# Two-bank PSUM tiles, two-head score evictions and halved key sums in an fp32 cross-attention block

## The chip, the cores and the metric

One core of a Trainium2 chip runs the whole block in one launch. The metric is the time of one execution in microseconds (us) on the device. Three runs of the kernel before took 665.59, 663.51 and 662.77 us; their median is 663.51.

The core has five engines with an instruction stream each: PE (TensorE, the matrix products; its weight loads are shown as PEld), DVE (VectorE), ACT (ScalarE), POOL (GpSimd) and SP (SyncE, which here only issues DMAs). Each works its stream off in order, and waits on semaphores where an operand comes from another engine. SBUF is the on-chip memory; PSUM holds what PE writes, in eight banks of 128 partitions x 512 fp32 numbers.

## The reference

A cross-attention block with an MLP, all in fp32: `x` is (8, 256, 512), `ctx` is (8, 256, 512), 16 heads of 32.

```python
h   = layer_norm(x, ln1_w, ln1_b)
q   = heads(h   @ q_w + q_b)          # (8, 16, 256, 32)
k   = heads(ctx @ k_w + k_b)
v   = heads(ctx @ v_w + v_b)
att = softmax(where(mask, q @ k.T * HD**-0.5, min)) @ v
hid = merge(att) @ cproj_w + cproj_b + x
y   = gelu(layer_norm(hid, ln2_w, ln2_b) @ fc_w + fc_b)   # (8, 256, 2048)
out = hid + y @ proj_w + proj_b
```

## The kernel before, in words

The eight batches are worked in two halves, g = 0 and 1, of four batches each, in one long program for one core. x and ctx are brought into columns by transposes on PE (`turned`, L709, the matmuls L725: `turn_c0_00` and so on) or through DRAM and DVE (`moved`, L730).

**Products.** Every projection (q, k, v, the output projection o, the MLP's fc and pd) is a Strassen-Winograd product: seven products of quarter operands in place of eight (`quad`, L857), the MLP with two levels of it. Each needs sums of quarters of its operands ahead (names like `c0t1`, `vws1`, `fw0i4_1`, `z1i2_3`, made by `plus`: DVE in one instruction of 1024 columns, L629, POOL in two halves of 512, L627) and sums of its results behind. The results come into PSUM banks called X, Y and W, and `take` (L601) brings them out, on DVE (L629) or on ACT (copies L605, with bias L610). All matmuls are issued at L638, save the transposes at L725 and the warming products at L650, which multiply a constant.

**Attention.** There are 32 units `u` = g, head group, batch: four heads x 256 queries x 256 keys each. `scores` (L1011) takes four one-bank buffers `s{u}_0` to `s{u}_3`, one to a head; a head's scores are keys x queries, in two halves of 128 keys. Eight instructions `ev{u}_jk` (j the head, k the key half; L1019 to L1021, issued by `copy`, L618, on ACT with the key's bias from `cols`) take 128x256 each to the SBUF buffers `pr{u}_0` and `pr{u}_1`, one to a pair of heads, each 128 keys x (2 heads x 2 key halves x 256 queries). Then come the maximum over keys (`mx`, DVE L1024, with `mt`, `mc` on ACT L1033, and `fold` L1034), its way through DRAM to all partitions (`md` out, `mm` back), the subtraction (`less`: DVE L1046 in one instruction of 1024, or POOL L1051 in two of 512) and the exponential (`exp`, ACT L1054). `attend` (L1061) multiplies with ones for the sums (eight matmuls, into the left half of a bank) and with v (eight matmuls, into the right half), and DVE divides (`r`: L1077, L1079, L1080; `att`, L629).

`scores` also has a second kind of unit, "z": there `ss` (L1055 to L1058) first adds the two key halves, as `ss{u}`, and `attend` needs four matmuls with ones in place of eight. In the kernel before, `KINDS` names no such unit.

**Order.** Nothing is scheduled on the chip. `PROGRAM` (L124) is one written list of all operations in order; a word is an operation's name, with a letter for the engine where there is a choice (`less000_0:G` on POOL, `:V` on DVE, `:A` on ACT). Each engine's stream is this list cut down to its own operations. `PLACES` (L350) gives each buffer its slot, and `Order.run` (L94) reads both. `BANKS` (L24) gives the PSUM banks: three of home W and five of home C. `tile_of` (L555) makes each bank one tile `[128, 512]`; a buffer waits until the one that had its bank before has been read.

The names used below: `s000` the score product of unit 000; `av000` its product with ones and v; `o1_0_P6` the sixth product of the output projection of half 1, column half 0; `fc015`, `pd06` parts of the two MLP products; `tq`, `rq` the output and the residual added to it at the end; `c0`, `cq0` the context of half 0 in columns and as loaded; `vw00` a quarter of v's weights.

Of the kernel before, what the change touches and what calls it, by code (L numbers as in the profile page):

```python
# [10 lines left out]
F32 = mybir.dt.float32  # L11
# [12 lines left out]
BANKS = {"W": 3, "C": 5}  # L24
# [19 lines left out]
class Order:  # L44
# [49 lines left out]
    def run(self):  # L94
# [30 lines left out]
cq0_00_1 cq0_00_0 vw00 rows1 cq0_01_1 vw11 vw10 cq0_01_0 turn_c0_10 turn_c0_00 kw00 c0_10:V small cq0_11_0 c0_00:A  # L125
cq0_10_1 rows6 v0_0_P1 rows4 cq0_11_1 vws1:G fw0_00_1 turn_c0_11 fw0_11_1 turn_c0_01 vws2:G rows0 c0_11:V v0_1_P1
c0_01:A kw10 v0_0_t1:A fw0_11_0 c0t1:V fw0_00_0 fw0_10_0 v0_1_t1:A cq0_10_0 turn_c0_31 turn_c0_21 c0_31:V k0_1_P1
c0_21:A c0t2:V rows3 fw0i1_1:G k0_0_P1 fw0_10_1 fw0i4_1:G xt0_0 v0_0_P6 rows8 fw0i4_2:V fw0i4_3:G kws3:V vw01 xt0_7
fw0i4_4:G v0_1_P6 kw11 v0_0_t2:V xt0_6 fw0i1_2:V kw01 fw0i1_4:V c0t3:V v0_0_P5 v0_1_t2:A mk fw0s1:V xt0_2 turn_c0_20
vws4:G fw1_01_1 turn_c0_30 stats_x0_00:V c0_20:A xt0_1 v0_1_P5 c0_30:A fw0s3:V xt0_4 fw0i5_1:G v0_0_P2 v0_1_t3:V  # L130
v0_0_t3:A rows7 kws1:G fw0s2:V xt0_3 fw0_01_0 v0_0_P3 fw0i6_1:V rows2 fw0i7_3:G stats_x0_30:V k0_1_P7 fw1_00_1
v0_0_c12:A xt0_5 stats_x0_31:V stats_x0_01:A fw1_00_0 mk~1 fw0i7_1:V fw1_11_1 v0_1_P2 fw0i6_2:V rows5 fw0i6_4:V
fw0i1_3:V fcd0_7_False stats_x0_11:A fw0i6_3:V qw00 vws3:V v0_1_P3 fw1_10_1 eps_x0_0:V stats_x0_10:V fw1_10_0 pow_x0_0
fcd0_4_True nb_x0_0 eps_x0_1:G fw0i7_2:V k0_1_P2 v0_1_c12:A fw0i7_4:G qw10 fw1i1_3:V stats_x0_20:A kws2:G
stats_x0_21:V cols k0_0_P7 fw1_01_0 cols~1 fcd0_5_False pow_x0_1 fw0i5_3:V k0_1_t1:A fw1_11_0 fw0i5_2:V eps_x0_2:G
k0_0_t1:A eps_x0_3:G k0_0_P2 kws4:V norm_x0_01:A pow_x0_3 fw0_01_1 qw11 pow_x0_2 k0_0_P6 k0_0_c11 fcd0_1_True fw1s3:V
xt1_3 k0_1_P6 nb_x0_3 nb_x0_2 fw1i1_1:V norm_x0_21:A k0_0_t2:V fw1i1_2:G norm_x0_31:A nb_x0_1 k0_0_P5 norm_x0_00:V
fw0i5_4:G k0_1_t2:A v0_0_c11 norm_x0_11:A fcd0_5_True fw1i4_1:V fw1i1_4:V fcd0_7_True norm_x0_30:A k0_1_P5 k0_0_t3:V
fcd1_1_True fw1i4_2:G k0_1_c11 fcd0_6_False fw1s1:G fw1i4_4:V k0_0_P3 k0_1_t3:A xt1_2 norm_x0_10:A k0_0_c22 xt1_0
norm_x0_20:A k0_1_P3 v0_1_c11 k0_0_c12:A fw1i4_3:V c0t4:V turn_x0_00 k0_1_c22 turn_x0_10 x0_00:A turn_x0_11 fw0s4:V  # L140
qw01 qws1:G turn_x0_01 x0_10:A fcd0_6_True turn_x0_20 x0_01:A x0_11:V k0_0_P4 xt1_1 fw1i2_1:V fcd1_5_False fcd1_4_True
fw1s2:V fw1i2_2:G turn_x0_31 k0_1_P4 x0_31:A x0t1:V fcd0_3_False turn_x0_21 fw1i2_4:V turn_x0_30 k0_1_c12:A fw1i2_3:V
q0_1_P1 k0_0_c21 qws2:G fcd1_2_True x0_20:A fcd1_6_False stats_x1_00 x0_21:A fw1i5_3:V fw1i6_1:G kd0_0_12 q0_0_P1
x0_30:A k0_1_c21 fcd1_7_False x0t2:V q0_0_P2 q0_0_t1:A x0t3:G qws3:V kd0_0_21 q0_0_P6 q0_0_c11 fw1i5_1:V cb1_02
fw1i6_3:G s000 q0_0_t2:A cb1_01 stats_x1_01 stats_x1_10 fw1i5_2:G kd0_0_11 q0_0_P5 ev000_20 stats_x1_11 fw1i6_2:G
ev000_10 ev000_00 fw1i5_4:G ev000_30 fw1i6_4:V ev000_01 q0_0_P7 fw1i7_1:G cb1_00 q0_0_t3:A q0_1_t1:A x0t4:G ev000_21
fcd1_5_True q0_1_P6 ev000_31 q0_0_c22 ev000_11 mx000_1 fcd1_6_True fw1i7_2:G q0_0_P4 mx000_0 cb1_12 fw0i2_3:G cb1_10
fw1i7_3:G aggr_x1_00 mt000 aggr_x1_01 kd0_0_22 fw0i2_1:V mc000_3 q0_1_P2 eps_x1_0:G mc000_2 q0_0_c21 mc000_1 fw0i2_2:V
aggr_x1_10 fold000 fw0i2_4:V s020 md000 cb1_11 qws4:G fcd0_2_True fw1s4:G q0_0_P3 cb1_30 ev020_01 q0_0_c12:V ev020_11
fw0i3_3:G fw0i3_1:V q0_1_t2:A fw1i3_3:G ev020_21 q0_1_P5 ev020_31 fw1i7_4:G ev020_30 ev020_00 fw0i3_2:G ev020_10 mm000  # L150
ev020_20 mx020_0 s002 cb1_32 vd0_0_12 v0_1_P7 ev002_30 cb1_03 aggr_x1_11 mx020_1 ev002_21 eps_x1_1:G pow_x1_0 ev002_00
cb1_31 ev002_20 fw1i3_1:G ev002_11 mt020 q0_1_P7 q0_1_c11 ev002_01 pow_x1_1 mc020_3 ev002_31 nb_x1_1 mc020_1
norm_x1_11:V mc020_2 fw1i3_2:V s022 v0_1_c22 fw1i3_4:G fold020 fw0i3_4:G v0_1_P4 nb_x1_0 mx002_1 md020 ev022_00
fcd1_3_True ev002_10 q0_1_t3:A less000_0:G cb1_13 ev022_10 mx002_0 ev022_31 v0_0_P7 ev022_20 ev022_01 ev022_21
q0_1_c22 norm_x1_10:A less000_1:G v0_1_c21 q0_1_P4 mm020 ev022_11 v0_0_c22 ev022_30 cb1_33 mt002 mx022_0 cb1_23 s010
cb1_22 exp000_1 q0_1_c21 cb1_20 v0_0_P4 mx022_1 cb1_21 mc002_1 mc002_2 fcd1_7_True ev010_01 cT1_00 ev010_20 xd1_3
ev010_00 cT1_10 q0_1_P3 mc002_3 ev010_10 kd0_1_12 less020_0:G cT1_11 ev010_31 exp000_0 cT1_01 k1_0_P1 fold002 v0_0_c21
norm_x1_00:A md002 fcd1_3_False q0_1_c12:V ev010_21 vd0_0_11 less020_1:G ev010_11 mt022 k1_1_P1 cT1_30 mc022_1 mc022_3
# [1347 lines left out]
```

## Time and profile before

| | |
|---|---|
| median of three runs | 663.51 us |
| lowest, highest | 662.77, 665.59 us |
| span of the profiled execution | 661.4 us |
| PE busy | 651.4 us, 98% |
| DVE busy | 571.6 us, 86% |
| POOL busy | 450.4 us, 68% |
| ACT busy | 356.5 us, 54% |
| DMA | 146.94 MB, mean 222 GB/s |

The profiled execution's own time isn't recorded apart from its span; the median stands 2.1 us above that span.

How to read the lines that follow. A line of a group reads: source line, engine, operation, out <- in by the program's names, partitions x elements of out and in, how many; then busy us and mean ns of one; then the idle time of the engine just before these instructions, and what ended most of it. A line of the windows gives, for a stretch of the span, each engine's busy us with the number of instructions, the clock granted to PE as a share of full speed, and the DMA engines' busy share and rate. A line of the waits reads: what was waited for, total us, times, longest. A line of the timeline gives start, length, engine, line, operation and how many alike stand in a row. A matmul instruction of fp32 shows as two records, so that a product with ones of eight matmuls stands as x16.

### The profile page before, as it was taken

The page shows a single profiled execution, that of the slowest core. Times are in us where ns is not written, and L with a number is a line of the kernel's source. Part 1 is how long each engine was busy: PE and PEld are TensorE (multiplying, and loading weights), DVE is VectorE, ACT ScalarE, POOL GpSimd, SP SyncE. Part 2 cuts the span into 40 slices and gives each one's busy share as a digit, 9 for nine tenths or more (in the row PEclk, how much of TensorE's full clock was granted, in tenths as well). Part 3 has the DMA queues.
Part 4 walks back from the last instruction along what each step waited for, and adds up shares of the span by engine and source line. Part 5 has one row for each costly group of instructions (what it writes and reads, how often), then busy time and mean ns, then how long its engine had stood idle before and what let it go on. Part 6 is the DMA issues. An engine that isn't in the chain of part 4 may idle for free.

```text
span 661.4 us, 11596 instructions
## 1 busy us (share of the span) xinstructions
PE 651.4 (98%) x3971; PEld 493.3 (75%) x3971; DVE 571.6 (86%) x935; ACT 356.5 (54%) x720; POOL 450.4 (68%) x397
## 2 busy tenths in 40 slices
PE   8999999999999999999999999999999999999997
PEld 6845464477545676787887878888888888888897
DVE  3989799879999999999989989987889779997573
ACT  2365698978989889837688890040222222730000
POOL 2476989868779996988999864659436046314882
PEclk9999999999999999999999999999999999999999
DMA  8999997889888568878555364979999995877256
GB/s 268 323 358 345 228 229 262 287 195 228 236 259 261 174 210 265 270 237 279 163 162 189 129 212 167 304 246 189 192 253 235 247 241 155 179 254 159 49 118 129
DMA packets 216538, 146.94 MB, mean 222 GB/s; under 512 B 125424, under 2 KB 176928, under 8 KB 216480
## 3 DMA queue, kind: packets, MB, share of 16 engines
q1 hardware_dynamic: 216480, 146.21, 78.9%
q8 instruction: 31, 0.51, 0.3%
q14 instruction: 27, 0.22, 0.1%
HBM read 105.67 MB, written 40.50 MB: 221 GB/s over the span
## 4 chain that ended last, share of the span: by engine, by line
PE 52%; DVE 5%; ACT 3%; DMA 1%; issue 1%; POOL 1%; SPq 0%; DVEq 0%
PE fc_X L638 14%; PE pd_X L638 14%; PE pd_W L638 7%; PE fc_W L638 6%; PE pd_Y L638 4%; PE fc_Y L638 3%; PE o_X L638 2%; DVE h L629 1%; PE av L638 1%; ACT pr L1054 1%; PE o_W L638 1%; ACT pr L618 1%; PE s L638 1%; DMA fl<-fcd 1%; DMA qw<-in_L_xattn_cproj_w_dram 1%
## 5 line engine op out<-in xcount | busy, mean ns | idle before, releaser
L618 ACT ACTIVATE pr<-s,cols 128x256 f32<-128x256 f32 x256 | 104.4, 483 | 17.4 <-PE s L638 10.6
L1051 POOL TENSOR_TENSOR pr<-pr,mm 128x512 f32<-128x512 f32 x72 | 98.4, 1393 | 7.7 <-DMA mm<-md 5.2
L1234 ACT ACTIVATE h<-h,cols 128x256 f32<-128x256 f32 x128 | 56.0, 499 | 55.7 <-DVE h L629 54.1
L1024 DVE TRANSPOSE_TENSOR_REDUCE mx<-pr 128x32 f32<-128x1024 f32 x64 | 77.5, 1222 | 2.5 <-ACT pr L618 2.4
L1054 ACT ACTIVATE pr<-pr 128x1024 f32<-128x1024 f32 x64 | 66.6, 1069 | 7.3 <-POOL pr L1051 4.1
L629 DVE TENSOR_TENSOR h<-fc_X,h 128x512 f32<-128x512 f32 x80 | 53.0, 679 | 7.1 <-PE fc_X L638 5.7
L1046 DVE TENSOR_TENSOR pr<-pr,mm 128x1024 f32<-128x1024 f32 x28 | 37.7, 1355 | 0.0
L629 DVE TENSOR_TENSOR h<-fc_W,h 128x512 f32<-128x512 f32 x48 | 32.1, 679 | 5.7 <-PE fc_W L638 5.5
L1033 ACT COPY mx<-mx 32x64 f32<-32x64 f32 x96 | 29.7, 309 | 11.9 <-DVE mx L1030 5.5
L638 PE MATMUL av<-pr,ones 128*32 128x256 f32 x512 | 34.1, 383 | 0.6 <-ACT pr L618 0.5
L610 ACT ACTIVATE e<-pd_X,cols 128x256 f32<-128x256 f32 x7 | 3.3, 471 | 57.0 <-PE pd_X L638 57.0
L629 POOL TENSOR_TENSOR h<-h,fl 128x512 f32<-128x512 f32 x9 | 12.3, 1368 | 25.7 <-DMA out_dram<-tq 22.4
L627 POOL TENSOR_TENSOR z1i<-z1t,z1i 128x512 f32<-128x512 f32 x8 | 10.0, 1270 | 25.5 <-DVE z1i L629 25.5
L638 PEld LDWEIGHTS av<-pr,ones 128*32 128x32 f32 x512 | 14.9, 109 | 16.1 <-issue 5.4
L638 PE MATMUL fc_W<-y1i,fl 128*128 128x256 f32 x100 | 24.5, 380 | 0.0
L638 PE MATMUL fc_X<-y1i,fl 128*128 128x256 f32 x88 | 22.5, 380 | 0.0
L638 PEld LDWEIGHTS fc_W<-y1i,fl 128*128 128x128 f32 x100 | 18.9, 190 | 2.9 <-DVE h L629 0.3
L605 ACT COPY h<-fc_X 128x512 f32<-128x512 f32 x16 | 9.1, 586 | 18.2 <-PE fc_X L638 14.2
L627 POOL TENSOR_TENSOR z1i<-h,z1i 128x512 f32<-128x512 f32 x10 | 13.4, 1362 | 7.8 <-ACT h L1234 4.1
L638 PE MATMUL pd_W<-z0i,pl 128*128 128x256 f32 x80 | 18.6, 379 | 0.0
L638 PEld LDWEIGHTS fc_X<-y1i,fl 128*128 128x128 f32 x88 | 16.7, 190 | 2.5 <-DVE h L629 0.3
L627 POOL TENSOR_TENSOR z0i<-h,z0i 128x512 f32<-128x512 f32 x10 | 16.3, 1653 | 1.4 <-DVE z0i L629 1.2
(601 smaller groups left out, 1905.6 us busy)
## 6 DMA issues: line engine op xcount, KB each, us to landing
mm<-md SPq DMA_DIRECT2D x32, 512.0 KB, 5.1
pl<-prd SPq DMA_DIRECT2D x54, 256.0 KB, 4.4
fl<-fcd SPq DMA_DIRECT2D x40, 256.0 KB, 4.5
fl<-prd SPq DMA_DIRECT2D x23, 256.0 KB, 4.6
fw<-in_L_xattn_fc_w_dram SPq DMA_DIRECT2D x16, 256.0 KB, 5.3
pw<-in_L_xattn_proj_w_dram SPq DMA_DIRECT2D x32, 128.0 KB, 4.2
hid<-in_x_dram SPq DMA_DIRECT2D x8, 512.0 KB, 7.8
hd<-hid SPq DMA_DIRECT2D x8, 512.0 KB, 3.9
```

The costliest lines, as they stand in the source:

```text
L605: (nc.scalar.copy if e == "ACT" else nc.vector.tensor_copy)(to(), of_())
L610: nc.scalar.activation(to(), of_(), AF.Identity, bias=bias(), scale=1.0)
L618: lambda e: nc.scalar.activation(to(), of_(), AF.Identity, bias=bias(), scale=1.0))
L627: nc.gpsimd.tensor_tensor(to()[:, ts(k, 512)], in0()[:, ts(k, 512)], in1()[:, ts(k, 512)], op)
L629: E[e].tensor_tensor(to(), in0(), in1(), op)
L638: nc.tensor.matmul(o(), l(), r(), start=first, stop=True, skip_group_check=True)
L1024: T.op(f"mx{u}_{h}", [("DVE", 1.126)], [(pr[h], None)], [(mx, [h])], lambda e, h=h: nc.vector.tensor_reduce(tile_of(mx)[:, 0:64].rearrange ...
L1033: lambda e, a=a: nc.scalar.copy(turned_()[0:32, 2 * a : 2 * a + 2, :], turned_()[32 * a : 32 * a + 32, 0:2, :]))
L1046: nc.vector.tensor_tensor(p_, p_, m_[:, :, None, :].to_broadcast([P, 2, 2, S]), ALU.subtract)
L1051: E[e].tensor_tensor(p_, p_, at(M, j)[:, None, :].to_broadcast([P, 2, S]), ALU.subtract)
L1054: lambda e, h=h: nc.scalar.activation(tile_of(pr[h]), tile_of(pr[h]), AF.Exp), table="exp")
L1234: lambda e, f=f, b=b, c=c: nc.scalar.activation(at(h[f][b], c), at(h[f][b], c), AF.Gelu_apprx_tanh, bias=col(c_fcb + f * 4 + c), scale=1.0 ...
```

## The change

- `BANKS` becomes four tiles of two banks each (S), whose halves serve as eight banks for everything else (W and C no longer differ). A buffer of kind S takes a whole tile.
- `scores` takes two S buffers `s{u}_0` and `s{u}_1` with two heads each. A unit is evicted by four instructions of 128 x 2 heads x 256 in place of eight.
- `KINDS` names six units "z": 000, 022, 012, 032 and 021 in half 0, 121 in half 1. Their twelve additions of key halves (128x512 each) are put five on DVE, seven on POOL.
- `PROGRAM` and `PLACES` are written anew: another order, other engines for some operations (on DVE 875 program instructions in place of 863, on POOL 296 for 293, on ACT 565 for 696, on PE the same 496 groups), other slots. The list holds no delays, before or now.

```diff
-BANKS = {"W": 3, "C": 5}
+BANKS = {"W": 8, "C": 8, "S": 4}
@@ Order.run
-                    w = where[b.name]
-                    b.home = w[0] if not w[0].isdigit() else b.kind
-                    b.slot = int(w.lstrip("WC"))
+                    b.slot = int(where[b.name])
@@ PROGRAM
-cq0_00_1 cq0_00_0 vw00 rows1 cq0_01_1 vw11 vw10 cq0_01_0 turn_c0_10 turn_c0_00 kw00 c0_10:V small cq0_11_0 c0_00:A
+vw00 cq0_00_1 cq0_00_0 cq0_01_1 cq0_01_0 cq0_11_1 rows7 cq0_11_0 cq0_10_1 cq0_10_0 small turn_c0_00 c0_00:V turn_c0_10
...
@@ KINDS
-KINDS = ("pppppppppppppppp", "pppppppppppppppp")
+KINDS = ("zppzppzzpzpppppp", "pppppppppzpppppp")
@@ tile_of
-    halves = {}
+    halves, sides = {}, {}
...
+            elif b.kind == "S":
+                b.t = banks.tile([P, 1024], F32, tag=f"B{b.slot // 2}", name=b.name)
+                sides[b.slot // 2] = None
             else:
-                b.t = banks.tile([P, 512], F32, tag=f"{b.home}{b.slot}", name=b.name)
+                s, k = divmod(b.slot, 2)
+                if sides.get(s) is None:
+                    sides[s] = banks.tile([P, 1024], F32, tag=f"B{s}", name=b.name)
+                b.t = sides[s][:, ts(k, 512)]
...
-    first = banks.tile([P, 512], F32, tag="W0", name="first")
+    first = banks.tile([P, 1024], F32, tag="B0", name="first")
@@ scores
-        sb = [Buf(f"s{u}_{j}", "C", 2) for j in range(4)]
+        sb = [Buf(f"s{u}_{h}", "S", 4) for h in range(2)]
         mm(f"s{u}", 1.076, [(q[0], None), (k[0], None)], [(s, None) for s in sb], [
-            (lambda kc=kc, j=j: at(sb[j], kc), lambda kc=kc, j=j: row(k, j)[:, ts(kc, P)], lambda j=j: row(q, j), True)
+            (lambda kc=kc, j=j: at(sb[j // 2], 2 * (j % 2) + kc), lambda kc=kc, j=j: row(k, j)[:, ts(kc, P)], lambda j=j: row(q, j), True)
...
-            for j in range(4):
-                copy(f"ev{u}_{j}{kc}", (pr[j // 2], [2 * (j % 2) + kc]), (sb[j], [kc]), lambda j=j, kc=kc: at(pr[j // 2], 2 * (j % 2) + kc),
-                     lambda j=j, kc=kc: at(sb[j], kc), 256, lambda kc=kc: col(2 * (4 * g + b) + kc))
+            for h in range(2):
+                both = lambda t, kc=kc: t.rearrange("p (i k q) -> p k i q", i=2, k=2)[:, kc]
+                copy(f"ev{u}_{h}{kc}", (pr[h], [kc, 2 + kc]), (sb[h], [kc, 2 + kc]), lambda h=h, both=both: both(tile_of(pr[h])),
+                     lambda h=h, both=both: both(tile_of(sb[h])), 512, lambda kc=kc: col(2 * (4 * g + b) + kc))
```

On PE, the place where unit 000 is multiplied with ones and v, before: `s030` is another unit's score product, with its four one-bank buffers, `av000` the unit's own bank.

```order
L638 MATMUL s030_0_1010<-xt0_4_389,k0_1_21_547 128x256
L638 MATMUL s030_1_1012<-xt0_4_389,k0_1_21_547 128x256
L638 MATMUL s030_2_1014<-xt0_4_389,k0_1_21_547 128x256
L638 MATMUL s030_3_1016<-xt0_4_389,k0_1_21_547 128x256
L638 MATMUL av000_1030<-pr000_0_722,ones_91 32x256 x2
L638 MATMUL av000_1030<-pr000_1_718,ones_91 32x256 x2
L638 MATMUL av000_1030<-pr000_0_722,v0_0_11_284 32x256 x2
L638 MATMUL av000_1030<-pr000_1_718,v0_0_11_284 32x256 x2
```

And the same place now. Where a half of a two-bank tile is written, the row has the name of the first buffer that lay in that tile (`v0_0_W`, `ps_c0_00`), and `ss000` is the sum of the two key halves.

```order
L624 MATMUL s012_0_979<-xn_x1_30_946,k0_1_12_604 128x256 x2
L624 MATMUL s012_1_982<-xn_x1_30_946,k0_1_12_604 128x256 x2
L624 MATMUL v0_0_W_807<-ss000_966,ones_91 32x256 x4
L624 MATMUL v0_0_W_807<-pr000_0_709,v0_0_11_350 32x256 x2
L624 MATMUL v0_0_W_807<-pr000_1_719,v0_0_11_350 32x256 x2
L624 MATMUL ps_c0_00_230<-pr020_0_776,ones_91 32x256 x2
```

The score product has two buffers in place of four, and the four rows with ones (each x2) of a unit have become one row x4 on `ss000`; the rows with v are the same.

On ACT, the evictions of unit 000's scores to `pr000_0` and `pr000_1`, before, with those of q products (rows L610, whose target stands in the slot of an old weight, `vw11`, or input, `xt0_7`) among them:

```order
L610 ACTIVATE xt0_7_334<-q0_0_X_673,cols_89 128x512
L618 ACTIVATE pr000_1_718<-s000_2_701,cols_89 128x256
L618 ACTIVATE pr000_0_722<-s000_1_699,cols_89 128x256
L618 ACTIVATE pr000_0_722<-s000_0_697,cols_89 128x256
L618 ACTIVATE pr000_1_718<-s000_3_703,cols_89 128x256
L618 ACTIVATE pr000_0_722<-s000_0_697,cols_89 128x256
L610 ACTIVATE vw11_215<-q0_0_X_673,cols_89 128x512
L610 ACTIVATE xt1_3_529<-q0_1_X_656,cols_89 128x512
L618 ACTIVATE pr000_1_718<-s000_2_701,cols_89 128x256
L618 ACTIVATE pr000_1_718<-s000_3_703,cols_89 128x256
L618 ACTIVATE pr000_0_722<-s000_1_699,cols_89 128x256
```

And now:

```order
L596 ACTIVATE vws1_301<-ps_c0_00_230,cols_89 128x512
L604 ACTIVATE pr000_0_709<-s000_0_699,cols_89 128x2x256
L596 ACTIVATE kws4_477<-ps_c0_00_230,cols_89 128x512
L604 ACTIVATE pr000_1_719<-s000_1_702,cols_89 128x2x256
L604 ACTIVATE pr000_0_709<-s000_0_699,cols_89 128x2x256
L604 ACTIVATE pr000_1_719<-s000_1_702,cols_89 128x2x256
L596 ACTIVATE xt0_1_291<-ps_c0_00_230,cols_89 128x512
```

Eight instructions of 128x256 have become four of 128x2x256, and two evictions with bias stand close to them as before, one of them now ahead of the first score.

On PE, the last attention unit ahead of the second output projection and the projection's first products, before: `av133` is the unit, `o1_0` and `o1_1` the projection, `att1` and `a1t2` its operand and the sums of it.

```order
L638 MATMUL av133_4110<-pr133_1_3933,ones_91 32x256 x2
L638 MATMUL av133_4110<-pr133_0_3920,vws1_255 32x256 x2
L638 MATMUL o1_1_X_4144<-fl013_3_3647,att1_00_2777 128x256 x4
L638 MATMUL o1_0_X_4161<-fl013_3_3647,att1_00_2777 128x256 x4
L638 MATMUL o1_0_Y_4179<-vws1_255,att1_10_3055 128x256 x4
L638 MATMUL o1_1_Y_4189<-vws1_255,att1_10_3055 128x256 x4
L638 MATMUL pd05_X_4197<-z0t1_0_3864,pl01_2_3777 128x256 x4
L638 MATMUL o1_1_X_4144<-fl017_3_3522,a1t2_4202 128x256 x4
L638 MATMUL o1_0_X_4161<-fl017_3_3522,a1t2_4202 128x256 x4
```

And now (the PSUM names are again those of first buffers: the rows with `att1` and `a1t` are the projection's):

```order
L624 MATMUL pd01_X_3607<-pr131_1_3439,ones_91 32x256 x2
L624 MATMUL pd01_X_3607<-pr131_0_3434,vw01_289 32x256 x2
L624 MATMUL pd01_X_3607<-h0_22_3160,pl05_2_3697 128x256 x4
L624 MATMUL fc004_Y_3557<-vws2_303,att1_00_2663 128x256 x4
L624 MATMUL fc005_X_3121<-z0t2_0_3713,v1_1_12_1641 128x256 x4
L624 MATMUL fc004_W_3637<-oxs2_3860,a1t2_3810 128x256 x4
L624 MATMUL fc004_Y_3557<-oxs2_3860,a1t2_3810 128x256 x4
L624 MATMUL fc004_W_3637<-ox10_3829,a1t1_3808 128x256 x4
```

The last unit is 131 in place of 133; one MLP product (`pl05_2`) now stands right ahead of the projection and another (`z0t2_0`) between its first product and those with `a1t2`; of the four rows with `att1` ahead of those only one is left there.

More of the change, by code (lines that the diff above doesn't have):

```diff
@@ L127 @@
[L127 to L146, printed above, removed]
@@ new lines @@
+ps_x0_00=0 x0_00=78 ps_x0_10=1 ps_x0_20=5 x0_10=8 ps_x0_30=7 ps_x0_01=1 x0_01=16 ps_x0_11=0 ps_x0_21=2 x0_11=74
+ps_x0_31=5 c0t1=54 c0t2=44 c0t3=80 c0t4=22 kw00=61 kw01=32 kw10=35 kw11=12 kws1=18 kws2=87 kws3=7 kws4=41 vw00=86
+vw01=37 vw10=28 vw11=53 vws1=82 vws2=71 vws3=20 vws4=29 qw00=36 qw01=56 qw10=40 qw11=65 qws1=44 qws2=43 qws3=45 qws4=42
+x0t1=4 x0t2=34 x0t3=88 x0t4=24 k0_0_X=3 k0_0_11=26 k0_0_Y=0 k0_0_21=19 k0_0_W=3 k0_0_22=77 k0_0_12=57 k0_1_X=4
+k0_1_11=76 k0_1_Y=6 k0_1_21=84 k0_1_W=6 k0_1_22=52 k0_1_12=14 v0_0_X=7 v0_0_11=64 v0_0_Y=1 v0_0_21=50 v0_0_W=0
```

617 lines of the change are left out of this document (307 added, 310 removed).

## The prediction

> **What bounds the kernel now.** I read the page first: its busy line and the clock row.
>
> ```profile
> span 661.4 us, 11596 instructions
> PE 651.4 (98%) x3971; PEld 493.3 (75%) x3971; DVE 571.6 (86%) x935; ACT 356.5 (54%) x720; POOL 450.4 (68%) x397
> PEclk9999999999999999999999999999999999999999
> ```
>
> PE is busy 98% of the span and its clock is granted in full in every slice, so PE's matmul time is the bound: the span shortens where PE gets less work, or where it waits less. The profiled execution's span is 661.4; the median of the three runs is 663.51, so 2.1 us lie around the span. I make the sum on the span and take it from the median. What a measurement of this kernel can tell from no change is about 0.5%, 3.3 us: faster means under 660.2, slower means over 666.8.
>
> An average says nothing of where the slack lies, so the windows came next, cut at the end of the head, where the attention units start, and where PE runs alone with the MLP.
>
> ```profile
> core 0: us, PE busy (x) PEld busy (x) DVE busy (x) ACT busy (x) POOL busy (x), PEclk, DMA share, GB/s
> 0.00:20.00 20.00, 17.43 (x104) 13.96 (x105) 7.75 (x10) 4.12 (x6) 6.56 (x14) 1.00 0.88 281
> 20.00:150.00 130.00, 129.91 (x741) 74.63 (x740) 115.33 (x201) 93.67 (x196) 96.76 (x92) 1.00 0.92 275
> 150.00:310.00 160.00, 156.78 (x1274) 107.06 (x1272) 154.00 (x257) 134.39 (x270) 137.16 (x126) 1.00 0.78 240
> 310.00:400.00 90.00, 89.58 (x621) 71.61 (x618) 82.88 (x134) 73.82 (x142) 76.85 (x61) 1.00 0.58 186
> 400.00:661.00 261.00, 257.72 (x1241) 226.05 (x1239) 211.64 (x337) 50.53 (x109) 133.06 (x107) 1.00 0.80 193
> ```
>
> Length less PE busy gives what PE waits: 2.6 in the head, 0.1, 3.2 from 150 to 310, 0.4, and 3.3 at the end. No better order can return more than these 9.6. DVE is the second bound: from 150 to 310 it is idle 6.0 of 160 us, from 310 to 400 it is idle 7.1 of 90, and from 20 to 150 it is idle 14.7 of 130, together 27.8. ACT is idle 25.6 and POOL 22.8 of the middle 160. The waits of PE say who it is that ends them.
>
> ```profile
> PE ps_c L725 <- DMA cq<-in_ctx_dram: 1.6, 2, 1.2
> PE o_X L638 <- DVE a0t L629: 1.0, 1, 1.0
> ...
> PE s L638 <- DVE q L629: 0.6, 1, 0.6
> PE av L638 <- ACT pr L618: 0.5, 2, 0.4
> PE fc_X L638 <- DVE h L629: 0.4, 2, 0.2
> PE ps_y L725 <- ACT pr L618: 0.3, 1, 0.3
> PE o_X L638 <- DVE a1t L629: 0.2, 1, 0.2
> PE fc_X L638 <- ACT h L605: 0.2, 1, 0.2
> ```
>
> Waits for DVE come to 1.0 + 0.6 + 0.4 + 0.2 = 2.2 us, those for ACT to 0.5 + 0.3 + 0.2 = 1.0.
>
> **The product with ones.** Where the work of PE itself changes is the six units whose sums take halved keys.
>
> ```profile
> 98.18 1.07 PE L638 MATMUL av<-pr,ones 128*32 128x256 f32 x16
> 99.07 1.05 PE L638 MATMUL av<-pr,v 128*32 128x256 f32 x16
> ```
>
> From start to start a unit's whole product with ones takes 99.07 - 98.18 = 0.89 us. Four of the eight matmuls go, 0.445 us, and six units make 2.7 us. This lies on the path, since PE waits for nearly nothing beside it: **-2.7**. No other matmul is added or dropped, so below this stand only waits.
>
> **Evictions of two heads.** ACT moves every score once, before in 256 instructions and now in 128 of twice the size.
>
> ```profile
> L618 ACT ACTIVATE pr<-s,cols 128x256 f32<-128x256 f32 x256 | 104.4, 483 | 17.4 <-PE s L638 10.6
> ```
> ```profile
> L618 ACT ACTIVATE att<-att,cols 128x512 f32<-128x512 f32 x16 | 11.4, 721 | 2.4 <-DVE att L629 2.3
> ```
> ```profile
> 244.98 1.99 ACT L1054 ACTIVATE pr<-pr 128x1024 f32<-128x1024 f32 x2
> ...
> 248.89 3.39 ACT L618 ACTIVATE pr<-s,cols 128x256 f32<-128x256 f32 x9
> ```
>
> Nine evictions in a row take 3.39, so each follows the last after (3.39 - 0.48) / 8 = 0.36 us. Two exponentials of 1024 take 1.99 where one takes about 1.06, a pitch of 0.93. Between 256 at 0.36 and 1024 at 0.93, 512 columns come to 0.55 as an estimate on the straight line: a unit takes 4 x 0.55 = 2.2 in place of 8 x 0.36 = 2.9, 0.7 us less, and 32 units 22 us. The other end is the 721 ns of a 512-wide row of the same form that shows no overlap: 4 x 0.72 = 2.9 and nothing is saved. I take the first, since the new instructions also stand in runs. ACT is at 54%, so neither is on the path; what the path gets is that ACT is late less often. I halve its 1.0 us of waits: **-0.5**, with 0 and -1.0 as bounds.
>
> The change adds a wait here: a score product now needs both banks of a pair, where it took single banks. What is queued behind it is everything, since PE works in order. How often a bank was not free before shows at PE's weight loads:
>
> ```profile
> PEld s L638 <- ACT pr L618: 5.2, 8, 0.8
> ```
>
> Eight times an eviction held up the load of a score product, 0.65 us each, and PE itself showed nothing of it under that name; the load ran ahead of a PE that was still at work. I take 0 for the pairs. The bounds are a further gain of nothing, as nothing was lost on PE, and a loss that the second rival prices.
>
> **DVE and POOL.** The twelve half-key adds go five to DVE and seven to POOL. The order also shifts work between the three engines: on DVE two more subtractions of the maximum, six more evictions of k and q sums, three fewer statistics of x, and seven fewer normalizations.
>
> ```profile
> L1051 POOL TENSOR_TENSOR pr<-pr,mm 128x512 f32<-128x512 f32 x72 | 98.4, 1393 | 7.7 <-DMA mm<-md 5.2
> ...
> L629 DVE TENSOR_TENSOR h<-fc_X,h 128x512 f32<-128x512 f32 x80 | 53.0, 679 | 7.1 <-PE fc_X L638 5.7
> L1046 DVE TENSOR_TENSOR pr<-pr,mm 128x1024 f32<-128x1024 f32 x28 | 37.7, 1355 | 0.0
> ```
> ```profile
> L629 DVE TENSOR_TENSOR c0t<-c,c 128x1024 f32<-128x1024 f32 x2 | 2.4, 1223 | 0.4 <-ACT c L605 0.4
> ```
> ```profile
> L627 POOL TENSOR_TENSOR c1t<-c,c 128x512 f32<-128x512 f32 x4 | 5.0, 1276 | 2.2 <-DVE c L749 2.2
> ```
>
> On DVE: 5 x 0.68 + 2 x 1.36 + 6 x 0.68 - 3 x 0.68 = 8.2; the rest (the normalizations, weight sums, operand sums, one to four instructions in each group) takes 4.8 away by the same means, so DVE has **+3.4 us** ahead of the second output projection. POOL gets 7 x 1.28 = 9.0 and gives two subtractions, in halves 2 x 2 x 1.39 = 5.6, to DVE. Neither is on the path where it can be placed in idle time: the 27.8 us of DVE and 22.8 of POOL. The order gives PE 6.3 us less matmul ahead of that same projection (2.7 of it saved, the rest moved behind it), so DVE must do 3.4 more in 6.3 less. That eats 9.7 of 27.8 and leaves 18: still cover, if it lies where it is needed. The worst stretch decides, so I looked for the run of DVE work that stands most over the PE work beside it: before 162.1 against 157.1, 5.0 over; after 142.5 against 138.4, 4.1 over. By these counts DVE forces less, and of the 2.2 us of waits for DVE I take off in proportion, 2.2 x 0.9 / 5.0 = **-0.4**. The bounds are -2.2 and the third rival.
>
> **Head.** `vw00` is now the first load, the eight context pieces follow, and all their turns but the first pair's stand ahead of the second v product.
>
> ```profile
> 10.10 1.07 PE L725 MATMUL ps_c<-ident,cq 128*128 128x128 f32 x8 [1.17 <-DMA cq<-in_ctx_dram]
> 11.01 1.89 PE L638 MATMUL v_X<-vw,c 128*128 128x256 f32 x8
> 12.74 1.08 PE L725 MATMUL ps_c<-ident,cq 128*128 128x128 f32 x8
> ```
>
> PE waits here for bytes. The wait of 1.17 can go, since the second pair of `cq0` is no longer split by `vw11` and `vw10`: -1.2 at most. On the other side `vw01` is now the twelfth large load, three behind the last context piece: 3 x 0.262 MB at the first window's 281 GB/s land in 2.8 us, and PE has a pair of turns (11.01 - 10.10 = 0.9) and a v product (12.74 - 11.01 = 1.7) to do meanwhile, 2.6. It nearly fits; a late load would cost what such waits cost here, 1.2, and 0.8 if it is the slower of two. I take 0, between -1.2 and +2.
>
> **Tail.** After the last product come an eviction, a transpose back and an add.
>
> ```profile
> L1334 DVE STREAM_TRANSPOSE tq<-po 128x256 f32<-128x256 f32 x32 | 12.8, 424 | 1.0 <-PE pd_X L638 0.8
> ```
> ```profile
> L629 POOL TENSOR_TENSOR tq<-tq,rq 128x512 f32<-128x512 f32 x9 | 11.9, 1330 | 7.1 <-DVE tq L1334 6.4 <-DVE h L629 0.6
> ```
> ```profile
> L629 DVE TENSOR_TENSOR po<-pd_X,po 128x256 f32<-128x256 f32 x20 | 8.3, 415 | 2.9 <-PE pd_X L638 2.6
> ```
> ```profile
> 647.29 1.78 PE pd_X L638 x16
> ```
>
> Ahead of the last products, POOL must add an output (1.33), then two operand sums (2 x 1.28 by the row of halves above): with the eviction and the transpose at 0.42 each, 4.7 us beside three products of 1.78 = 5.3. It fits by 0.6; I take 0, bound +1.
>
> **Sum.** -2.7 - 0.5 - 0.4 + 0 + 0 = -3.6: a span of 657.8 and a time of 663.5 - 3.6 = **659.9**.
>
> **The rivals.** *Pairs of banks.* The four tiles are scarcer than eight banks where score products meet projections; a product that waits for the second bank stops PE. For it speaks the weight-load row above; against it, that the two evictions that freed one bank now free both of a pair. With half of those eight cases, 4 x 0.65 = 2.6 us, reaching PE, the time is 662.5. It decides from about 0.3 us on, where the sum passes 660.2.
>
> *Adds become the bound: slower.* The place is from 150 to 400 us. There the half-key adds have two inputs in SBUF, on both engines, and so have the subtractions. The subtractions, at 1355 against 1223 ns on DVE and 1393 against 1276 on POOL, show 0.12 to 0.13 us of a shared cost each. If DVE sets the time up to the second output projection, PE comes to it 3.4 later than before, whatever it saved, and has 3.6 us of matmul more behind it: 663.5 + 7.0 = 670.5; with half of it, 667.0. It decides once the idle time of DVE from 20 to 400 doesn't come down from 27.8 to below 21 while PE waits for `less`, `ss` or operand sums. Against it stands the worst stretch, 4.1 where it was 5.0. The sharpest form is that each new POOL add stops DVE for its whole 1.28: 7 x 1.28 = 9.0, and 672.5; the 0.13 us of the rows are a tenth of that, so of the slower case I give this form 0.03. The Trainium skill (SBUF — State Buffer, section "Who interferes with whom") holds the rule for it and so speaks against this change: a DVE instruction with two SBUF inputs contends with a GpSimd instruction that reads SBUF, and the one that comes second is blocked outright. By that rule, the rows agree in sign only.
>
> *Nothing happens.* If the six units wait for `ss` as long as they save, the time is 663.5 - 0.9 = 662.6. The adds come between the exponentials and the product and take 0.7 (DVE) or 1.3 us (POOL), but products of other units and projections stand between, so I give it little.
>
> **How the numbers follow.** The sum stands only 0.3 under the line of 660.2, and its case is not all on one side. Its case (the sum right to within its bounds, 656.0 to 662.5) has 0.60: 0.46 below the line, since what I put at nothing in the order is bounded by idle time that it may take back (656.0 is the median less 2.7, less the 3.6 of waits from 150 to 400, less 1.2 of the head), and 0.14 above. Bank pairs have 0.16, nothing happens 0.06: both within 0.5%. Slower has 0.18, half of it over 667.0. So faster is 0.46, same 0.36, slower 0.18. The range is **656.0 to 667.0**: it leaves out the upper half of the slower case, 0.09, and about as much below and between.
>
> **What would show it.** Right: the product with ones at half its count in six units, PE's busy time 2.7 lower, waits of PE for ACT at 0.5, ACT busy 22 lower, the DVE idle from 20 to 400 near 18, no wait of PE for a score eviction over 1 us in sum. Wrong: waits of `s` for `pr` evictions of several us (pairs), or waits of PE for DVE's and POOL's `pr` and `ss` from 150 to 400 of over 4 us (adds), or `ps_c` and `v_X` waits over 4 us in the head.

## The result, and the profile after

The changed kernel takes 806.22 us (median of four runs, 805.68 to 809.11), the kernel before 663.43 on the same chip: a ratio of 1.216, 95% interval 1.213 to 1.219. Forecast were 659.9 and a range up to 667.0. The prediction was wrong by 146 us, and none of its cases held this.

The page of the changed kernel, in the rows that answer to those of before:

```profile
span 804.4 us, 11349 instructions
...
PE 690.4 (86%) x3923; PEld 504.4 (63%) x3923; DVE 579.5 (72%) x944; ACT 343.3 (43%) x603; POOL 442.7 (55%) x398
...
PEclk9999989999999998899999999999999999999999
```

DVE, ACT and POOL have about the work that they had: 579.5 us for 571.6, 343.3 for 356.5, 442.7 for 450.4. They are busy a smaller share of a longer span, so none of them has become the bound. PE is idle 804.4 - 690.4 = 114 us, where it was idle 10, and its busy time has grown by 39 us for 48 records less. The windows, cut as before:

```profile
core 0: us, PE busy (x) PEld busy (x) DVE busy (x) ACT busy (x) POOL busy (x), PEclk, DMA share, GB/s
...
20.00:150.00 130.00, 119.11 (x633) 64.05 (x631) 106.25 (x182) 78.42 (x138) 88.01 (x86) 0.97 0.84 260
150.00:310.00 160.00, 132.68 (x1000) 86.29 (x1000) 123.04 (x206) 109.01 (x181) 103.24 (x94) 0.96 0.61 172
310.00:400.00 90.00, 69.44 (x415) 51.80 (x416) 55.05 (x98) 36.61 (x58) 49.36 (x53) 0.89 0.53 176
400.00:804.00 404.00, 353.00 (x1775) 289.45 (x1773) 287.19 (x453) 110.56 (x208) 197.89 (x157) 0.97 0.64 158
```

From 310 to 400 each of the four engines is idle for a good part: PE 21 of 90 us, DVE 35, ACT 53, POOL 41, though hardly ever all at once (0.1 us of the 90, by the trace). That is the picture of engines that wait for each other in turn, not of a bound. It is no matter of one stage either: after 400 PE loses another 51 of 404. The waits of PE:

```profile
PE fc_X L624 <- DVE h L615: 10.9, 9, 2.5
PE ps_y L624 <- DVE h L615: 8.3, 2, 4.3
PE pd_X L624 <- DVE h L615: 7.7, 7, 2.3
PE av L624 <- DVE rc L1064: 6.1, 1, 6.1
...
PE s L624 <- DVE xt L615: 3.8, 2, 2.9
...
PE s L624 <- DVE h L615: 0.9, 1, 0.9
```

Score products (`s`), the only ones that need both banks of a tile, wait little: with 0.5 for an eviction (`pr`), 5.2 us of PE's 114. And the waits of DVE, to be laid beside the first:

```profile
DVE h L615 <- PE fc_X L624: 21.1, 15, 4.7
DVE h L615 <- PE ps_y L624: 12.1, 6, 5.9
```

PE waits for DVE to read PSUM, and DVE waits for PE to write it. One case shows how. The timeline of PE, and then that of DVE, around the longest wait:

```profile
304.93 1.03 PE L624 MATMUL ps_y<-y0i,fl 128*128 128x256 f32 x4
312.10 2.08 PE L624 MATMUL av<-y,qws 128*128 128x256 f32 x4 [6.14 <-DVE rc L1064]
```
```profile
305.18 0.42 DVE L615 TENSOR_TENSOR att<-av,r 128x256 f32<-128x256 f32 x1 [2.04 <-ACT vws L813]
...
307.91 2.33 DVE L1033 TENSOR_TENSOR pr<-pr,mm 128x1024 f32<-128x1024 f32 x1
...
311.65 0.40 DVE L1064 TRANSPOSE_TENSOR_REDUCE rc<-av 128x8 f32<-128x256 f32 x1
```

In the program the product of 312.10 and the reduction it waits for are these rows:

```
PE   L624 MATMUL av100_2492<-y0_00_2575,qws1_538 128x256 [waits DVE_49]
DVE  L615 TENSOR_TENSOR att1_00_2663<-av100_2492,r100_2621 128x256 [waits DMAHW7_49,Activation_49]
DVE  L1064 TENSOR_REDUCE rc110_2670<-av100_2492 128x8
```

`av100` is the name of a two-bank tile. The product is an MLP product that writes its left bank, columns 0 to 255. The last reader of that bank is `att1_00`, which ended at 305.6. The reduction `rc110` reads the sums of another unit, columns 768 to 1023, in the right bank. It shares no number with the product, but it shares the tile, and the product waits for it: 6.1 us, behind a subtraction of 2.33, two reductions and the queue ahead of them. In the whole program 106 waits of PE are of this sort, for a read of the *other* bank of a tile (80 for DVE, 26 for ACT), and some 95 reads of DVE and ACT wait for a product written to the other bank. These are counts of the program's rows, not of the trace; the program before has none of either.

### The profile page after: what moved, and what is told of

Read it like the earlier page. It is cut to its first block, busy times and chain, and to the rows that moved or that the text cites. A ratio compares the mean times of both kernels' runs of the same rounds, so it can differ in the third digit from the quotient of the medians.

```text
span 804.4 us, 11349 instructions
## 1 busy us (share of the span) xinstructions
PE 690.4 (86%) x3923; PEld 504.4 (63%) x3923; DVE 579.5 (72%) x944; ACT 343.3 (43%) x603; POOL 442.7 (55%) x398
## 5 line engine op out<-in xcount | busy, mean ns | idle before, releaser
L1038 POOL TENSOR_TENSOR pr<-pr,mm 128x512 f32<-128x512 f32 x68 | 88.7, 1329 | 38.7 <-DMA mm<-md 37.3
L604 ACT ACTIVATE pr<-s,cols 128x512 f32<-128x512 f32 x128 | 81.7, 686 | 51.2 <-PE s L624 49.3
L615 DVE TENSOR_TENSOR h<-fc_X,h 128x512 f32<-128x512 f32 x50 | 33.8, 680 | 22.3 <-PE fc_X L624 20.2
L1033 DVE TENSOR_TENSOR pr<-pr,mm 128x1024 f32<-128x1024 f32 x30 | 38.1, 1280 | 1.1 <-DMA mm<-md 1.1
L613 POOL TENSOR_TENSOR z0i<-z0t,z0t 128x512 f32<-128x512 f32 x8 | 12.8, 1620 | 33.3 <-DVE z0t L615 31.5
L615 DVE TENSOR_TENSOR h<-fc_Y,h 128x512 f32<-128x512 f32 x33 | 22.2, 682 | 8.8 <-PE fc_Y L624 7.7
L615 DVE TENSOR_TENSOR h<-pd_X,h 128x512 f32<-128x512 f32 x26 | 17.6, 680 | 7.2 <-PE pd_X L624 6.5
L615 POOL TENSOR_TENSOR tq<-tq,rq 128x512 f32<-128x512 f32 x8 | 10.1, 1268 | 17.9 <-DMA rq<-hd 13.1
L613 POOL TENSOR_TENSOR z0t<-h,z0t 128x512 f32<-128x512 f32 x10 | 15.3, 1552 | 5.9 <-PE fc_Y L624 3.0
L624 PE MATMUL fc_Y<-z0i,pl 128*128 128x256 f32 x48 | 13.1, 422 | 3.5 <-DVE po L615 2.8
L624 PE MATMUL av<-pr,ones 128*32 128x256 f32 x240 | 15.9, 382 | 0.3 <-ACT pr L604 0.3
```

The source lines that it names most:

```text
L604: lambda e: nc.scalar.activation(to(), of_(), AF.Identity, bias=bias(), scale=1.0))
L613: nc.gpsimd.tensor_tensor(to()[:, ts(k, 512)], in0()[:, ts(k, 512)], in1()[:, ts(k, 512)], op)
L615: E[e].tensor_tensor(to(), in0(), in1(), op)
L624: nc.tensor.matmul(o(), l(), r(), start=first, stop=True, skip_group_check=True)
L1033: nc.vector.tensor_tensor(p_, p_, m_[:, :, None, :].to_broadcast([P, 2, 2, S]), ALU.subtract)
L1038: E[e].tensor_tensor(p_, p_, at(M, j)[:, None, :].to_broadcast([P, 2, S]), ALU.subtract)
```

## The experiments

The theory after this reading is **sharing**: four tiles of two banks make halves wait for each other. Its rivals are the **order** (adds and DVE, the slower rival of the prediction) and the **evictions of two heads** by themselves. Ten kernels were run.

**1. The change's order on one-bank tiles.** The same physical banks, engines and list; each bank a tile; the scores evicted one head at a time, at the same places.

```diff
...
-    sides[s] = banks.tile([P, 1024], F32, tag=f"B{s}", name=b.name)
-    b.t = sides[s][:, ts(k, 512)]
+    b.t = banks.tile([P, 512], F32, tag=f"B{b.slot}", name=b.name)
...
```

> The changed kernel with the same order, the same engines, the same six units with halved key sums and the same physical banks, but every bank a tile of its own and the scores evicted one head at a time. Theory (sharing): a tile of two banks makes a product for one bank wait until the other bank has been read (106 such waits of PE on DVE or ACT), and a read of one bank wait for a product written to the other; without them the forecast's terms are left, 663.4 - 2.7 - 0.4 = 660.3, with 0.5 either way, so 659 to 663. Rival (order): the new order and the adds on DVE and POOL have made DVE the bound; then it stays near 800. Rival (a change of this kind hidden in the evictions of two heads) can't be told from the first theory here: both give about 660.

Measured: 677.2 us (672.6 to 682.0), ratio 1.019 (1.015 to 1.023). The 143 us are gone but for 13. The order can't be the cause of the loss, but the forecast's 660 isn't there either. That miss is taken up in 5.

**2. The same without halved sums.** The words `ss` are taken out of the list as well.

```diff
-KINDS = ("zppzppzzpzpppppp", "pppppppppzpppppp")
+KINDS = ("pppppppppppppppp", "pppppppppppppppp")
```

> The kernel above without the halved key sums: no unit adds its key halves, all 32 products with ones have eight matmuls. Sharing theory with the forecast's terms: 6 x 0.445 = 2.7 us slower than the kernel above, about 663. If the adds on DVE and POOL take back what PE saves, it is equal or faster than the kernel above. If the order were at fault, again near 800.

Measured: 678.4 (676.9 to 681.2), ratio 1.021 (1.018 to 1.024). Slower by 1.2 with intervals that overlap: inconclusive; the question is put again in 6.

**3. The kernel before on four two-bank tiles.** Nothing but the tiles is changed.

```diff
-    b.t = banks.tile([P, 512], F32, tag=f"{b.home}{b.slot}", name=b.name)
+    s, k = divmod(b.slot + (3 if b.home == "C" else 0), 2)
+    if sides.get(s) is None:
+        sides[s] = banks.tile([P, 1024], F32, tag=f"B{s}", name=b.name)
+    b.t = sides[s][:, ts(k, 512)]
...
```

> The kernel before, order and evictions untouched, with its eight banks made into four tiles of two banks each (neighbours by number: W0 with W1, W2 with C0, C1 with C2, C3 with C4). Sharing theory: it has 121 waits of PE for a read of the other bank, where the changed kernel has 106, so it loses about as much: 143 x 121 / 106 = 163, some 825 us; anything from 760 to 900 speaks for it. Rivals (order, adds, evictions of two heads): nothing of theirs is in this kernel, so 663.

Measured: 760.4, ratio 1.144 (1.139 to 1.149). Its page:

```profile
PE 685.3 (90%) x3971; PEld 495.5 (65%) x3971; DVE 582.4 (77%) x935; ACT 360.8 (47%) x720; POOL 444.1 (58%) x397
```

This is the signature of the change without its order, adds or evictions: with a span of 759.6 PE is idle 74 us, and it is busy 34 us longer at the same 3971 records. Its score products still take single banks, so the loss doesn't need a product that wants a whole pair. The size, 96.5, is below the 163 that went by the number of waits, at the lower edge of what was named: a wait costs what the other bank's reader happens to be late, and a count of waits doesn't give that.

**4. One pair only, and the change with eight evictions.** The dose: of the kernel before, only the banks C3 and C4 in one tile.

```diff
-    b.t = banks.tile([P, 512], F32, tag=f"{b.home}{b.slot}", name=b.name)
+    s = b.slot + (3 if b.home == "C" else 0)
+    if s < 6:
+        b.t = banks.tile([P, 512], F32, tag=f"B{s}", name=b.name)
+    else:
+        if sides.get(0) is None:
+            sides[0] = banks.tile([P, 1024], F32, tag="B67", name=b.name)
+        b.t = sides[0][:, ts(s - 6, 512)]
...
```

> The kernel before with two of its eight banks (C3 and C4) made into one tile, the other six tiles of their own: 30 waits of PE for a read of the other bank in place of 121 with four pairs. Sharing theory: the loss of four pairs, 760.4 - 663.9 = 96.5, in that proportion is 24 us, so about 688; between 672 and 700 speaks for it. If only the sum of all pairs stalled PE (a pool that runs dry), one pair costs nothing, 663.

Measured: 693.2, ratio 1.044 (1.041 to 1.047), 29 us for one pair of four. So it is no pool that runs dry at the fourth pair; a single shared tile costs already. And the other rival, in the change itself, each place of an eviction in the list taking two:

```diff
-            for h in range(2):
-                copy(f"ev{u}_{h}{kc}", (pr[h], [kc, 2 + kc]), (sb[h], [kc, 2 + kc]), ..., 512, ...)
+            for j in range(4):
+                copy(f"ev{u}_{j}{kc}", (pr[j // 2], [2 * (j % 2) + kc]), (sb[j // 2], [2 * (j % 2) + kc]), ..., 256, ...)
```

> The changed kernel with its two-bank tiles, but the scores evicted one head at a time, eight instructions of 128x256 to a unit, two of them at each place of the list. Sharing theory: the 106 waits of PE are all there, so 800 to 815, a little above the changed kernel's 806 since ACT has 22 us more to do. Rival (the two-head evictions themselves hold up PE): it comes back to about 665.

Measured: 809.8, ratio 1.219 (1.213 to 1.224). Evictions one head at a time bring nothing back. Sharing is the cause of the loss; the two-head evictions are not.

**5. Where the other 13 us of the first kernel went.** One-bank tiles leave ACT eight evictions to a unit. This kernel gives ACT four again, a whole bank each, by leaving out the second half's mask bias:

```diff
-            for j in range(4):
-                copy(f"ev{u}_{j}{kc}", ..., 256, lambda kc=kc: col(2 * (4 * g + b) + kc))
+            for h in range(2):
+                j = 2 * h + kc
+                copy(f"ev{u}_{h}{kc}", (pr[h], [2 * kc, 2 * kc + 1]), (sb[j], None), ..., lambda j=j: tile_of(sb[j]), 512, ...)
```

> The changed kernel's order, engines, units and banks, every bank a tile of its own, but four evictions to a unit again, each of one head's whole bank, 128x512. They take the bias of the first key half for both halves, so the mask's bias of the second half is left out. The time of ACT is thus that of the change, without its two-bank tiles. If the 13 us by which the order on one-bank tiles was slower than before come from ACT's eight evictions, which the order wasn't written for, this runs at 659 to 663, the forecast. If they come from the order itself (loads, DVE, POOL), it stays at 672 to 678.

Measured: 666.3 (663.0 to 669.8, nine runs), ratio 1.0035 (1.0011 to 1.0059). It lies between the two expectations: 10.9 of the 13 were ACT's eight evictions, and with four the order stays a little behind before. Against the change, this kernel differs by its tiles, by the bias, and by the shape of the evictions (one head's two halves in place of one half of two heads, 128x512 both), so sharing costs 806.2 - 666.3 = 140 us, as far as the bias and the shape cost nothing (ACT's evictions take the same time in both, 686 and 684 ns). The same edit in the kernel before, where the list keeps the first of a bank's two evictions and drops the other:

> The kernel before with four evictions to a unit, each of one head's whole bank, 128x512, at the place of the bank's first one; they take the bias of the first key half for both, so the mask's bias of the second half is left out. It is the forecast's term for fewer evictions alone: -0.5, between 0 and -1.0, so 663; ACT is busy some 22 us less. If the longer instructions hold a bank's reader up, it is slower by a few us.

Measured: 662.7, ratio 0.998 (0.996 to 0.9994). Its waits of PE; the three for ACT are gone:

```profile
PE o_X L638 <- DVE a0t L629: 1.1, 1, 1.1
PE first L650 <- DVE warm L645: 1.0, 1, 1.0
PE ps_c L725 <- DMA cq<-in_ctx_dram: 0.8, 1, 0.8
PE fc_X L638 <- DVE h L629: 0.4, 2, 0.2
PE o_X L638 <- DVE a1t L629: 0.2, 1, 0.2
```

**6. The halved sums.** In the change's order, the kernel of 5 with the edit of 2:

> The change's order on one-bank tiles with four evictions of one head's whole bank (the mask's bias of the second key half left out), and without the halved key sums: eight matmuls with ones in all 32 units, no adds of key halves. The forecast's term by itself, in the order that was written for it: this is 2.7 us slower than the same kernel with the six units (666.3), so about 669. Rival: the adds take back what PE saves, so it is equal or faster, 663 to 666.

Measured: 670.1 (665.4 to 673.0), ratio 1.0079 (1.0054 to 1.0105). Between the ratios with and without lies 0.0044, 2.9 us, with intervals that overlap at their ends: the size that was forecast, though hardly clear of the noise. In the kernel before, with the adds on DVE, half way between exponential and product:

```diff
-KINDS = ("pppppppppppppppp", "pppppppppppppppp")
+KINDS = ("pzppzzzppzpzpppp", "pppppppppppppppp")
-av000 fold022 mx010_1 md022 xd1_0 vd0_0_21 ev030_01
+av000 ss020_0:V fold022 mx010_1 md022 ss020_1:V xd1_0 vd0_0_21 ev030_01
```

> The kernel before with six units (020, 010, 030, 012, 021, 023) that add their key halves, all twelve adds on DVE, the rest of the order untouched. It is the forecast's term for the product with ones alone: -2.7, so 661, if DVE has room for 12 x 0.68 = 8.2 us more in its idle time. Rival: DVE is the bound there and gives the adds back, 663 to 668.

Measured: 673.1, ratio 1.015 (1.012 to 1.017), the rival's side and past it. The waits of PE:

```profile
PE s L629 <- ACT pr L1045: 3.7, 1, 3.7
PE av L629 <- DVE ss L620: 2.7, 3, 1.9
```

And with four early units and the adds late:

```diff
+KINDS = ("pzppzzzppppppppp", "pppppppppppppppp")
-av000 fold022 mx010_1 md022 xd1_0 vd0_0_21 ev030_01 mt010 av020
+av000 fold022 mx010_1 md022 xd1_0 vd0_0_21 ss020_0:V ev030_01 ss020_1:V mt010 av020
```

> The kernel before with four units that add their key halves (020, 010, 030, 012), all ahead of 150 us, where DVE was idle 14.7 of 130, and with the eight adds on DVE late between the exponential and the product with ones, so that DVE does not stand waiting for the exponential. If the 9 us that six units cost came from DVE waiting in its queue and from the two later units, this gains 4 x 0.445 = 1.8 and runs at 662. If DVE has no room even there, 665 to 670.

Measured: 669.6, ratio 1.0075 (1.0051 to 1.0099): slower again, with the rival's number. The adds themselves are now what PE waits for:

```profile
PE av L628 <- DVE ss L619: 3.9, 3, 1.9
```

In a list that wasn't written for them the adds cost more than the product saves, in both places that were tried (all of them on DVE, where the change puts seven of its twelve on POOL). How much of it is PE's wait for the adds (2.7 and 3.9 us are shown) and how much is what stands behind them in DVE's queue was not separated; the expectation that the early stretch has room was wrong. So the 2.7 us were seen only with an order that makes room. Of the kernels run that compute the whole block, none is faster than the kernel before.

## Why the prediction was wrong, point by point

**The step that failed** is the one on pairs of banks. The prediction says of the evictions' change that "a score product now needs both banks of a pair" and takes 0 for it, with a rival of 2.6 us. It saw the tile only as a thing that score products must find empty. It didn't ask what a PSUM tile is for every *other* product: the unit in which the program orders writes after reads. 232 buffers, the results of the projections, of the MLP and of the transposes and the products with ones and v, live in halves of these tiles. The diff says so in five lines (`sides[s][:, ts(k, 512)]`), and the order of the changed kernel shows the same tile name under unrelated products, as the rows quoted with the change do (`v0_0_W` for unit 000's product). That was read as a matter of names. Had one wait of such a row been followed to its reader, the other bank would have been found. A count of waits wouldn't have told it: the order of the changed kernel has PE wait for DVE 220 times in place of some 250, but 80 of the 220 are for a reader of the wrong bank. The sign that the prediction had named for this rival, waits of `s` for `pr` evictions of several us, never came: they are 0.5 us in the changed kernel. It watched the right tiles and the wrong products; the term of 0, and 2.6 in the rival, measured 140.

**What the loss is made of.** Beside the kernel of 5, with the same records, PE has 690.4 - 650.0 = 40 us more busy time and 114 - 14.5 = 99.5 us more idle time, together 140. The page of that kernel:

```profile
span 664.5 us, 11397 instructions
...
PE 650.0 (98%) x3923; PEld 493.0 (74%) x3923; DVE 583.2 (88%) x944; ACT 342.7 (52%) x603; POOL 457.0 (69%) x398
```

Of the 40, some 27 are PE's clock: by the windows above, 119 x 0.03 + 133 x 0.04 + 69 x 0.11 + 353 x 0.03 comes to that, where the clock was 1.00 in every window before. It is lowest, 0.89, where the waits are longest (6.14, and 4.3 for `ps_y`). The chain shows what one wait of 2.44 us, ahead of 671.64, does:

```profile
670.29 1.30 DVE h L615 x2
671.64 1.13 PE fc_Y L624 x4
672.77 1.65 PE pd_X L624 x4
674.41 1.71 PE fc_Y L624 x4
676.12 1.79 PE fc_X L624 x8
...
678.77 0.86 PE fc_W L624 x4
```

The first product behind it takes 1.13 us in place of 0.86 and the next two take 1.65 and 1.71, twice as long; the clock granted from 672.7 to 676.1 was 0.50. Then two products take 1.79, and all is as before. In the kernel of 3 a wait of 1.93 us (79.1 to 81.0) was enough:

```profile
78.70:82.10 3.40, 1.47 (x4) 0.59 (x4) 1.37 (x2) 2.17 (x6) 3.09 (x5) 1.00 1.17 298
82.10:85.50 3.40, 3.40 (x19) 1.32 (x17) 2.63 (x5) 1.07 (x3) 1.27 (x3) 0.51 1.05 200
```

The Trainium skill (TensorE: Matmul & The Clock Gate, Part 1) says that the clock falls to half once PE has been idle for about 3.4 us. That it falls to half behind a gap the traces agree with; the size of the gap they don't bear out, since no wait in the kernel of 3 was over 2.5 us. About 3.4 us long is here the stretch at half clock, in both places above.

The other 13 us are of the size of the first product behind a wait: 0.27 us more for each of the 62 waits of PE that this kernel has above the kernel of 5 (83 for 21) would be 17. That part is argued, not tried. In the kernel of 3 it is the larger one: of its 34 us more, the clock of its windows (0.99, 0.97, 1.00 and 0.99 from 20 us on) explains some 8.

**The product with ones: right, as well as the runs can tell.** Each of the six products takes 0.456 us by its starts in the kernel of 5, in place of 0.89; six times the difference is 2.6, and the kernels of 5 and 6 lie 2.9 us apart by their ratios. In the pair of 1 and 2 it was 1.2, inside the noise.

**Evictions: right in kind.** The pitch of the large eviction is 0.57 us against the estimate of 0.55, by the starts of runs such as this one of the changed kernel:

```profile
L604 ACT ACTIVATE pr<-s,cols 128x512 f32<-128x512 f32 x128 | 81.7, 686 | 51.2 <-PE s L624 49.3
...
141.10 2.40 ACT L604 ACTIVATE pr<-s,cols 128x512 f32<-128x512 f32 x4
```

(2.40 - 0.69) / 3 = 0.57. The group's busy time fell from 104.4 to 81.7 us, the 22 of the prediction; ACT's as a whole fell by 13 only. The term of -0.5 measured -1.3 in the order before, with an interval (0.4 to 2.7 us) that holds the forecast, and -10.9 in the order that counts on it.

**DVE and POOL: the rival was not it, the sum was not either.** The twelve adds and the shifted work are in the kernel of 5 too, and it is 2.3 us slower than before. Its windows:

```profile
20.00:150.00 130.00, 128.03 (x703) 72.64 (x702) 120.08 (x202) 88.89 (x157) 97.07 (x95) 1.00 0.92 284
150.00:310.00 160.00, 156.76 (x1277) 108.14 (x1276) 153.24 (x263) 120.81 (x196) 133.27 (x121) 1.00 0.74 225
310.00:400.00 90.00, 88.74 (x594) 70.71 (x594) 83.52 (x131) 78.67 (x133) 66.55 (x53) 1.00 0.62 192
```

9.9 + 6.8 + 6.5 = 23, in place of 27.8 before and the 18 of the forecast: not below the 21 under which the rival was to be out. But PE shows no wait there for `less`, `ss` or operand sums, which the rival needed too, and the time is not its 667 to 670 either. Nor is it the 672.5 of its sharpest form; what that form got right is told in the last section. What does show is that the order by itself, without halved sums and with four evictions (670.1), is behind the kernel before with four evictions (662.7) by (1.0079 - 0.9977) x 664 = 6.8 us, where the prediction gave it -0.4 and put head and tail at 0. The waits of PE in the profiled run of the first:

```profile
PE ps_c L705 <- DMA cq<-in_ctx_dram: 2.0, 1, 2.0
PE av L618 <- ACT pr L598: 1.8, 1, 1.8
PE s L618 <- ACT pr L598: 1.6, 2, 1.0
PE av L618 <- ACT pr L1035: 1.5, 2, 0.8
PE fc_W L618 <- DMA fl<-fcd: 1.1, 1, 1.1
PE pd_W L618 <- DMA pl<-prd: 1.0, 1, 1.0
```

ACT is waited for 4.9 us and two loads of MLP operands come late (2.1), none of which the kernel before with four evictions shows, and the head waits 2.0 where that one waits 0.8, inside its bounds. That is 8.2 us. It can't be set against the 6.8 as it stands, since the profiled run took 672.95, above its kernel's median of 670.1 (the spans of the two profiled runs, 671.2 and 660.5, lie 10.7 apart), but it says of which kind the loss is. The count of DVE work by which the term was made (162.1 and 142.5 us up to a product, figures that no view here shows) held none of it: it compared totals, and what is late is single instructions on ACT and single transfers. Which words of the list make them late was not tried.

**The result as a sum**, by the kernels: sharing +140, the order +6.8, the halved sums -2.9, the evictions -1.3: 142.6, against 806.2 - 663.4 = 142.8 measured. The kernels are steps of one chain, so their differences must come to about the whole; that they do proves none of them. The forecast's parts were 0, -0.4, -2.7 and -0.5.

## What to carry to other kernels

A PSUM tile was here not only a place, but the unit in which the program orders its writes behind its reads. (SBUF tiles, which both kernels share by halves too, were not looked at.) Before two things are put into one tile to save instructions, list every other user of that tile and follow a wait or two to the instruction that ends it; a wait for an instruction that shares no number with the waiting one is a price that no count of waits shows. Where one transfer or eviction wants two banks, the gain (here 1.3 us before, 10.9 in an order that needs it) has to be set against all products that come to live in the halves (here 140 us). And an operation that is cheap by its duration, like the adds of key halves, is only cheap where the list has a place for it: six units with halved sums were worth -2.9 us in one order; in the other, four and six units, with all adds on DVE, cost 5 and 9.

## What the runs showed of the hardware that was not expected

- PE's granted clock, 1.00 in every window of the kernel before, fell to a mean of 0.961 on one core when PE waited often. It fell to half for about 3.4 us behind single waits of 2.44 and 1.93 us too. A stall of PE thus costs more than its length: 27 of the 143 us.
- A block between DVE and POOL, both with two SBUF inputs, is whole in a few instructions, and the means hide it. The prediction read the means of the subtractions, 1355 ns on DVE and 1393 on POOL, as a shared cost of 0.12 to 0.13 us each. By least, median and longest most of them cost nothing more:

```profile
L1046 DVE TENSOR_TENSOR pr<-pr,mm x28: 1169/1216/2068, 106.2 to 388.3; 128x1024 f32<-128x1024 f32 x28
L1051 POOL TENSOR_TENSOR pr<-pr,mm x72: 1256/1273/2523, 83.6 to 338.4; 128x512 f32<-128x512 f32 x72
```

  The subtraction of 2.33 us on DVE (307.91) in the changed kernel's longest wait is such a one. It started 0.02 us behind a subtraction on POOL, whose two halves, 1.27 us each by the median, took 3.47:

```profile
307.89 3.47 POOL L1038 TENSOR_TENSOR pr<-pr,mm 128x512 f32<-128x512 f32 x2
```

  Against the median of 1.22 that kernel's DVE lost 1.1 us there, about what was left of POOL's first half, and POOL's second lost about as much. The rule of the Trainium skill that the prediction weighed (SBUF — State Buffer, "Who interferes with whom") is borne out by this, in size and not in sign only. Its price in time was not taken apart: in the changed kernel, with both engines idle more, the means were 1280 and 1329.
- An eviction that reads two banks at once, 128 x 2 x 256, keeps the pitch of one that reads a single bank: 0.57 us in the changed kernel and in that of 5. The pair costs ACT nothing. The Trainium skill (PSUM — Partial Sum Buffer, section "PSUM bank collisions raise a hardware error") asks for an order of writes and reads by bank; the changed program keeps it by pairs, and that is where the time went.
- Two kernels with the new order spread more than the kernel before in the same sessions: 672.6 to 682.0 in six runs of the first, 665.4 to 673.0 in nine runs of the last one without halved sums, against 662.5 to 666.8 in 11 and 662.6 to 666.6 in 14 runs of before. Two others hardly did: 676.9 to 681.2 in six runs of the second, and 663.0 to 669.8 in nine of the kernel of 5 against 662.8 to 668.4 in 18 of before. Where the spread arises was not tried.
